# Folding the output projection ahead of the first normaliser, and holding the last band's taps until the third band

## The chip, the cores and the metric

The kernel runs on one NeuronCore of one Trainium2 chip. The metric is the device time of one execution in microseconds (us); lower is better. The engines are TensorE (PE in the profile, with its weight loads as PEld), VectorE (DVE), ScalarE (ACT), GpSimd (POOL) and SyncE (SP, which issues most DMAs).

## The reference

Eight images of 384 channels and 64 x 64 pixels, all in float32, go through two residual layers. Each layer starts with a group normalisation over 32 groups (`_gn`).

```python
# layer 0: linear attention, 6 heads of 64
q = apply_rope_2d(conv1x1(xn, Wq, bq)); k = apply_rope_2d(conv1x1(xn, Wk, bk)); v = conv1x1(xn, Wv, bv)
q = elu(to_heads(q) * scale) + 1;  k = elu(to_heads(k)) + 1
kv = einsum('bhnd,bhne->bhde', k, v);  k_sum = k.sum(axis=2)
normalizer = einsum('bhnd,bhd->bhn', q, k_sum)
out = einsum('bhnd,bhde->bhne', q, kv) / (normalizer + 1e-6)
x = x + conv1x1(out, Wfc, bfc)
# layer 1: spectral filter, depthwise convolution, gate
t = einsum('bchw,oc->bohw', _gn(x), w_in)
t = irfft2(rfft2(8x8 patches of t) * fft_filter)
t = depthwise 3x3 convolution of t with w_dw, zero-padded
x1, x2 = halves of t's channels
x = x + einsum('bchw,oc->bohw', gelu(x1) * x2, w_out)
```

## The kernel before, in words

**Tiles.** An image is held as channels on partitions: 3 tiles (CT = 3) of 128 channels. Its 4096 pixels are cut into 8 bands of 8 rows (NBAND = 8), 512 pixels each. A band of activations is a tile of 128 x 3 x 512 float32.

**Stages.** A loop runs over the images b. For each, `queries` works the second half of layer 0, band by band. Then a loop over the bands works layer 1, filled up with the keys and values of image b+1. Work is laid out with Python generators that are advanced by hand (`next`, `run`); from that the framework's scheduler makes, when the program is built, a fixed order for each engine. Engines wait for each other with semaphores.

**A band in `queries`.** These steps follow each other, and different bands are in different steps at once:
- `q_project`: TensorE makes pq (L597, 18 matmuls in two or three groups); DVE multiplies it with the tables of the rotary embedding (the "turns", L610, L625), ScalarE makes the third tile's swapped half (qs, L624), DVE adds (L626). `elu_plus_one` then is ScalarE's relu and exp (L337, L338) and a last DVE step (L339) on the tile qc.
- `q_normalise`: TensorE multiplies qc with ks_bd (pn, L635); DVE takes the reciprocal (L644) and splits it in parts for a bf16 matmul, with two casts on ScalarE (L648, L650).
- `q_spread`: TensorE spreads the parts over the channels (prb, L659), and DVE multiplies qc with them in four pieces (L668).
- `project_out`: TensorE makes pf from qc and mt (L676, in two pieces: the first 6 matmuls and the other 12), DVE adds it to x (L680).

**The fold.** The output projection needs mt, the product of the image's kv matrix (kvt) and Wfc. `kv_finish_heads` makes kvt: ScalarE copies the accumulated matrix to kx (L566), POOL puts the key sums into ks_bd with 12 small copies (L498), DVE makes kvt_bd (L571), TensorE transposes it (pt, L583), and ScalarE copies it to kvt (L584). Its last step is `fold`: TensorE makes pm (L508) and nine copies bring it to mt, five on ScalarE (L515) and four on DVE (L513). In `queries` the rest of that generator, with the fold, runs after the projection of band 2, and pn_0 is ahead of it.

**The last band of the image before.** In layer 1 a band's depthwise convolution has 3 tiles x 9 taps. The first tap is made by ScalarE (`first_taps`, L776); the other eight are DVE steps that accumulate in the tile dw (`tile_taps`, L787), 24 in a band. Then come the gate (L799 to L804) and `contraction` (pw, L820 and L831), whose result ScalarE copies to y (L845) and POOL adds into the output in DRAM with an accumulating DMA (L850). Band 7 of image b-1 is not finished in its own stage: `last_band` is a generator, handed to `queries(b)` as `late`. Each `next(late, None)` in the loop over j (from j = 2 on) is one step: the taps of tile 0, of tile 1, of tile 2 with the gate, and the contraction. The weights are in `w_dw`, in SBUF since the start, so the scheduler is free to start these DVE steps as soon as DVE has room; in the order that it made, 13 of the 24 taps of band 7 stand between 985 and 1013 us of the profile, among the steps of bands 0, 1 and 2. There are seven such boundaries, one for each image but the first.

**Buffers.** The band tiles qc, qs, kx, kvt and others come from one pool of 9 (`w_tile`); a new tile waits for the last use of the one that it replaces. The tiles dw come from a pool of two. PSUM has eight tiles (`ps_tile`).

**Loads.** x of the image after comes through SP's queue in the order in which it is written; bands 0 and 1 are loaded at j = 5 and j = 6 of `queries`.

Of the kernel before, what the change touches and what calls it, by code (L numbers as in the profile page):

```python
# [9 lines left out]
F32 = mybir.dt.float32  # L10
BF16 = mybir.dt.bfloat16
AF = mybir.ActivationFunctionType
ALU = mybir.AluOpType

P = 128
C = 384
CT = 3
H = W = 64
N = H * W
NBAND = 8  # L20
# [97 lines left out]
def conv_blocks_kernel(ctx: ExitStack, tc: tile.TileContext, a: dict, out: bass.AP, nb: int):  # L118
    nc = tc.nc
# [6 lines left out]
    small = ctx.enter_context(tc.tile_pool(name="small", bufs=2))  # L126
    psum = ctx.enter_context(tc.tile_pool(name="psum", bufs=8, space=bass.MemoryType.PSUM))

    def ps_tile(name):
        return psum.tile([P, 512], F32, tag="ps", name=name)  # L130

    def w_tile(shape, name):
        return work.tile(shape, F32, tag="w", name=name)
# [6 lines left out]
    def load_x(b, j):  # L140
        if b >= nb:
            return
        t = xp.tile([P, CT, BT], F32, tag="x", name=f"x_{b}_{j}")
        nc.sync.dma_start(t, x_in[b][:, :, j * BT : (j + 1) * BT])
        xt[b, j] = t
# [96 lines left out]
    ident = groups[:, 2 * CT * NG :]  # L242
# [4 lines left out]
    scale = HD ** -0.5  # L247
# [9 lines left out]
    ring = []  # L257
# [245 lines left out]
    def fold(b, kvt, wfc, done):  # L503

        mt = small.tile([P, CT, C], F32, tag="mt", name=f"mt_{b}", bufs=1)
        for t in range(CT):
            pm = ps_tile(f"pm_{b}_{t}")
            nc.tensor.matmul(pm[:, :C], kvt[:, t, :], wfc[:, t, :], start=True, stop=True)  # L508
            for i, (c, at, n) in enumerate(QPIECES):
                if c // P == t:  # L510
                    dst, src = mt[at % P : at % P + n, at // P, :], pm[c % P : c % P + n, :C]
                    if i % 2:
                        nc.vector.tensor_copy(dst, src)  # L513
                    else:
                        nc.scalar.copy(dst, src)  # L515
        done.append(mt)
# [113 lines left out]
    def q_normalise(b, j, q):  # L630

        pn = ps_tile(f"pn_{b}_{j}")
        for t in range(CT):
            for s in range(4):
                nc.tensor.matmul(  # L635
                    pn[32 * s : 32 * s + 32, :P],
                    ks_bd[:, t, :],
                    q[:, t, s * P : (s + 1) * P],
                    start=(t == 0),
                    stop=(t == CT - 1),  # L640
                )
        rn = small.tile([P, P], F32, tag="rn", name=f"rn_{b}_{j}")
        nc.vector.tensor_scalar_add(rn, pn[:, :P], 1e-6)
        nc.vector.reciprocal(rn, rn)  # L644

        part = small.tile([P, P], BF16, tag="part", name=f"part_{b}_{j}")
        parts = small.tile([P, P], BF16, tag="parts", name=f"parts_{b}_{j}")
        nc.scalar.copy(part, rn)  # L648
        nc.vector.scalar_tensor_tensor(rn, part, take_off[:, 0:1], rn, ALU.mult, ALU.add)
        nc.scalar.copy(part, rn)  # L650
        nc.vector.scalar_tensor_tensor(parts, part, take_off[:, 1:2], rn, ALU.mult, ALU.add)
        return parts

    def q_spread(b, j, q, rn):
        pr = [ps_tile(f"prb_{b}_{j}_{s}") for s in range(4)]
        for t in range(CT):
            for s in range(4):
                strip = slice(32 * s, 32 * s + 32)
                nc.tensor.matmul(  # L659
                    pr[s][:, t * P : (t + 1) * P],  # L660
                    expand[strip, t * P : (t + 1) * P],
                    rn[strip, :],
                    start=True,
                    stop=True,
                )
        for s in range(4):
            qq = q[:, :, s * P : (s + 1) * P]
            nc.vector.tensor_mul(qq, qq, pr[s][:, :C].rearrange("p (t n) -> p t n", t=CT))  # L668
# [80 lines left out]
    dw, dw_pe, diagonals = {}, {}, []  # L749

    def on_array(b, j):

        return b == nb - 1 and j >= NBAND - 2
# [7 lines left out]
    def array_taps(b, j, ks):  # L761

        for k in ks:
            nc.tensor.matmul(
                dw_pe[b, j].rearrange("p (r w) -> p r w", w=W),
                diagonals[0][:, k * P : (k + 1) * P],
                ring[j % 2][:, 2, k // 3 : k // 3 + 8, k % 3 : k % 3 + W],
                start=(k == 0),
                stop=(k == 8),
            )  # L770

    def first_taps(b, j):

        acc = dw[b, j] = taps_pool.tile([P, CT, 8, W], F32, tag="dw", name=f"dw_{b}_{j}")
        for m in range(CT - on_array(b, j)):
            nc.scalar.activation(acc[:, m], ring[j % 2][:, m, 0:8, 0:W], AF.Copy, scale=w_dw[:, m, 0:1])  # L776
        if on_array(b, j):
            dw_pe[b, j] = ps_tile(f"ptap_{b}_{j}")
            array_taps(b, j, range(9 if j == NBAND - 1 else 6))

    def tile_taps(b, j, m):

        t, acc = ring[j % 2], dw[b, j]
        for k in range(1, 9):
            src = t[:, m, k // 3 : k // 3 + 8, k % 3 : k % 3 + W]
            wd = w_dw[:, m, k : k + 1]
            nc.vector.scalar_tensor_tensor(acc[:, m], src, wd, acc[:, m], ALU.mult, ALU.add)  # L787

    def taps(b, j):
        if on_array(b, j) and j < NBAND - 1:  # L790
            array_taps(b, j, range(6, 9))
        for m in range(CT - on_array(b, j)):
            tile_taps(b, j, m)

    def gate_taps(b, j):
        g = gated
# [58 lines left out]
    def layer0_chain(b, prepared):  # L855

        if b >= nb:
            return
        wk = load_weight(b, "wk", k_runs) if b else first_wk
        params = []  # L860
        if b == 0:
            sum_weight(wk, "wk")
        yield from norm_chain(b, 0, params)
        scale_weight(wk, params)
        yield
        prepared += params, wk, k_bias(b, params)
# [5 lines left out]
    def run(*chains):  # L872

        chains = list(chains)
        while chains:
            chains = [c for c in chains if next(c, chains) is not chains]
# [65 lines left out]
    def queries(b, keys, before_last, late):  # L942


        wq, qbias = keys.wq, keys.qbias
        q, done, normaliser = {}, [], {}

        def normalise(j):
            normaliser[j] = q_normalise(b, j, q[j])

        run(q_project(b, 0, wq, qbias, q))
        before_last()
        run(keys.accumulate(NBAND - 1))
        finish = keys.finish(done)
        for _ in zip(q_project(b, 1, wq, qbias, q), finish):
            pass
        prepared = []
        chain = layer0_chain(b + 1, prepared)

        normalise(0)  # L960
        run(q_project(b, 2, wq, qbias, q))
        run(finish)
        mt = done[0]
        q_spread(b, 0, q[0], normaliser.pop(0))
        project = q_project(b, 3, wq, qbias, q)
        next(project)
        normalise(1)
        run(project)
        output_ = project_out(b, 0, q.pop(0), mt)
        next(output_)  # L970
        q_spread(b, 1, q[1], normaliser.pop(1))
        normalise(2)
        run(output_)
        for j in range(2, NBAND):
            if j < NBAND - 2:
                project = q_project(b, j + 2, wq, qbias, q)
                for _ in range(2):
                    next(project)
                normalise(j + 1)
                run(project)  # L980
                next(chain, None)
            q_spread(b, j, q[j], normaliser.pop(j))
            output_ = project_out(b, j - 1, q.pop(j - 1), mt)
            if j == NBAND - 2:
                next(output_)
                normalise(j + 1)
            run(output_)
            if j < NBAND - 2:
                next(chain, None)
            if j == 5:  # L990
                load_x(b + 1, 0)
            next(late, None)
            if j == 6:
                load_x(b + 1, 1)
        run(chain)
        run(project_out(b, NBAND - 1, q.pop(NBAND - 1), mt))
        return prepared
# [14 lines left out]
    for c0, at, n in QRUNS:  # L1012

        t, p0, quarter, first = at // P, at % P, c0 // QC, c0 % QC
# [13 lines left out]
    w_dw = const_tile([P, CT, 9], "w_dw", a["w_dw"], nc.sync)  # L1028
# [30 lines left out]

    def last_band(b):  # L1060

        for m in range(CT):
            tile_taps(b, NBAND - 1, m)
            if m == CT - 1:
                gate_taps(b, NBAND - 1)
            yield
        if b + 1 < nb - 1:
            contract(b, NBAND - 1)

    before_last, late = nothing, iter(())  # L1070
    for b in range(nb):
# [52 lines left out]
        def before_last(b=b):  # L1124
            contract(b, NBAND - 2)

        late = last_band(b)


    make_diagonals()  # L1130
    b = nb - 1
# [60 lines left out]
```

## Time and profile before

| | before |
|---|---|
| time, median of 3 runs | 3383.83 us (3383.71 to 3386.06) |
| the profiled execution: time, span | 3384.08 us, 3382.3 us |
| mean granted TensorE clock | 0.992 of full speed |
| PE busy | 3300.6 us |
| DVE busy | 2786.1 us |
| ACT busy | 1965.9 us |
| POOL busy | 142.6 us |
| fold's copies on DVE (L513), one | 551 ns |
| fold's copies on ACT (L515), one | 472 to 475 ns |
| a tap on DVE (L787), one | 748 ns |
| a first tap on ACT (L776), one | 756 ns |
| y's accumulating DMA, 768 KB, issue to landing | 7.8 us median, 7.6 to 9.6 |
| loading of an activation table on ACT, one | 1.28 us |

A row of a group reads: line, engine, operation, output and inputs with their shapes, count, busy time and mean duration of one, and then the idle time of the engine just before these instructions, with the instruction that ended it. A row of the list of waits reads: what waited, what it waited for, microseconds in total, how often, the longest. A row of the timeline reads: start, duration, instruction, count, and the idle time before it. Durations on one engine overlap by some 0.08 us, so that a tap of 748 ns takes 0.66 us of DVE's time in a row of taps. In rows by windows, the number behind POOL is the granted clock of TensorE.

### The profile page before, as it was taken

The numbers are of one execution on the slowest core, as the hardware profiler recorded it, in microseconds if no ns is written. First come the engines' busy times: TensorE is split into PE (matmuls) and PEld (weight loads), VectorE is DVE, ScalarE is ACT, GpSimd is POOL, SyncE is SP. The second block draws the span as 40 slices with busy tenths as digits, with TensorE's granted clock in tenths as the row PEclk, the third lists the DMA queues.
The fourth block names the chain that finished last, engine by engine and source line by source line (L and its number), as shares of the span: only waits on it lengthen the run. The fifth ranks groups of instructions, "written<-read, shape, count | busy, mean of one in ns | idle before, by whom it ended". The sixth has DMA issues, their size and how long they took to land.

```text
span 3382.3 us, 53235 instructions
## 1 busy us (share of the span) xinstructions
PE 3300.6 (98%) x21356; PEld 1850.2 (55%) x21356; DVE 2786.1 (82%) x4438; ACT 1965.9 (58%) x3849; POOL 142.6 (4%) x247
## 2 busy tenths in 40 slices
PE   8999999999999999999999999999999999999987
PEld 5544565456654566545664456644566445664454
DVE  6587889968899688996889868898788977989598
ACT  4445675556665576655675556655576555555553
POOL 0000001000010000100001000010000100000000
PEclk9999999999999999999999999999999999999999
DMA  6323244242442423424334333433233431324113
GB/s 223 112 94 108 75 101 111 100 138 56 111 115 94 135 74 87 123 101 120 85 89 122 102 115 76 111 109 116 92 96 93 120 114 54 85 70 112 57 24 53
DMA packets 149483, 336.01 MB, mean 99 GB/s; under 512 B 27140, under 2 KB 38388, under 8 KB 141044
## 3 DMA queue, kind: packets, MB, share of 16 engines
q1 hardware_dynamic: 123844, 282.85, 24.9%
q0 software_dynamic: 25200, 49.55, 10.1%
q8 instruction: 168, 2.75, 0.3%
q14 instruction: 79, 0.65, 0.1%
q10 hardware_dynamic: 192, 0.21, 0.0%
HBM read 232.70 MB, written 99.88 MB: 98 GB/s over the span
## 4 chain that ended last, share of the span: by engine, by line
PE 82%; DVE 14%; ACT 2%; issue 1%; DMA 0%; SPq 0%; DVEq 0%; ACTq 0%
PE pf L676 15%; PE pk L438 14%; PE pi L694 13%; PE pv L454 13%; PE pq L597 9%; DVE dw L787 6%; PE pw L820 4%; PE pb L729 3%; PE pd L708 2%; PE pw L831 2%; PE acc L470 2%; PE acc L483 2%; PE pn L635 1%; DVE qc L610 1%; DVE qc L339 1%
## 5 line engine op out<-in xcount | busy, mean ns | idle before, releaser
L787 DVE SCALAR_TENSOR_TENSOR dw<-ring,w_dw,dw 128x512 f32<-128x512 f32 x1520 | 1063.1, 748 | 244.2 <-ACT ring L745 205.4
L597 PE MATMUL pq<-x,wq 128*128 128x512 f32 x1152 | 529.0, 607 | 27.9 <-ACT qs L624 16.9
L438 PE MATMUL pk<-wk,x 128*128 128x384 f32 x1536 | 543.6, 495 | 0.0
L694 PE MATMUL pi<-w_in,hf 128*128 128x384 f32 x1536 | 514.4, 492 | 1.3 <-ACT hf L332 1.3
L676 PE MATMUL pf<-qc,mt 128*128 128x512 f32 x1152 | 512.8, 598 | 0.2
L454 PE MATMUL pv<-wv,x 128*128 128x384 f32 x1344 | 470.0, 488 | 0.0
L694 PEld LDWEIGHTS pi<-w_in,hf 128*128 128x128 f32 x1536 | 288.4, 191 | 196.0 <-issue 3.8
L438 PEld LDWEIGHTS pk<-wk,x 128*128 128x128 f32 x1536 | 282.9, 190 | 204.6 <-issue 31.3
L597 PEld LDWEIGHTS pq<-x,wq 128*128 128x128 f32 x1152 | 213.0, 192 | 278.9 <-issue 241.1
L461 ACT COPY v<-pv 128x384 f32<-128x384 f32 x224 | 108.7, 485 | 423.9 <-PE pv L454 416.3
L454 PEld LDWEIGHTS pv<-wv,x 128*128 128x128 f32 x1344 | 253.6, 190 | 181.4 <-issue 8.4
L676 PEld LDWEIGHTS pf<-qc,mt 128*128 128x128 f32 x1152 | 213.6, 190 | 253.7 <-issue 238.8
L680 DVE SCALAR_TENSOR_TENSOR x<-pf,bfc,x 128x512 f32<-128x512 f32 x192 | 140.8, 744 | 121.4 <-PE pf L676 121.3
L337 ACT ACTIVATE qs<-qc 128x1536 f32<-128x1536 f32 x64 | 95.0, 1485 | 169.7 <-DVE qc L626 148.6
L820 PE MATMUL pw<-gated,w_out 128*128 128x256 f32 x768 | 179.9, 384 | 0.0
L441 DVE TENSOR_TENSOR kc<-pk,kbias 128x384 f32<-128x384 f32 x256 | 141.0, 551 | 38.5 <-PE pk L438 38.2
L179 ACT ACTIVATE differences<-x,shift 128x512 f32<-128x512 f32 x168 | 119.7, 713 | 86.4 <-DVE x L680 86.4
L701 ACT COPY ht<-pi 128x384 f32<-128x384 f32 x256 | 115.0, 482 | 92.0 <-PE pi L694 88.7
L820 PEld LDWEIGHTS pw<-gated,w_out 128*128 128x128 f32 x768 | 146.9, 192 | 37.1 <-issue 6.5
L624 ACT ACTIVATE qs<-pq,qbias 64x512 f32<-64x512 f32 x128 | 87.4, 683 | 123.8 <-DVE qc L610 122.6
L850 POOL DMA_DIRECT2D out_dram<-y x63 | 80.7, 1281 | 1849.0 <-ACT y L845 847.1
L337 ACT ACTIVATE ks<-kc 128x1536 f32<-128x1536 f32 x64 | 95.0, 1485 | 98.6 <-DVE kc L445 69.5
(171 smaller groups left out, 4360.9 us busy)
## 6 DMA issues: line engine op xcount, KB each, us to landing
tq<-in_tq SPq DMA_DIRECT2D x64, 1024.0 KB, 4.8
x<-in_x SPq DMA_DIRECT2D x64, 768.0 KB, 5.9
tk<-in_tk SPq DMA_DIRECT2D x64, 768.0 KB, 4.4
out_dram<-x SPq DMA_DIRECT2D x63, 768.0 KB, 3.3
out_dram<-y POOLq DMA_DIRECT2D x63, 768.0 KB, 7.8
xs<-in_x SPq DMA_DIRECT2D x56, 768.0 KB, 5.9
wk<-in_wk SPq DMA_DIRECT2D x8, 576.0 KB, 3.8
wfc<-in_wfc SPq DMA_DIRECT2D x8, 576.0 KB, 7.9
```

The source lines that it names most:

```text
L179: nc.scalar.activation(out[:, m, :], x_[:, m, :], AF.Identity, bias=shift[:, m : m + 1], accum_out=of_m[0])
L337: nc.scalar.activation(e, x_, AF.Relu, scale=-1.0)
L438: nc.tensor.matmul(pk[:, :C], tokens(t), wks[:, t, :], start=(t == 0), stop=(t == CT - 1))
L441: nc.vector.tensor_add(kc[:, i, :], pk[:, :C], bias)
L454: nc.tensor.matmul(pv[:, :C], xt[b, j][:, t, i * P : (i + 1) * P], wvs[:, t, :], start=(t == 0), stop=(t == CT - 1),)
L597: nc.tensor.matmul(p_, wqs[:, t, m * P : (m + 1) * P], xt[b, j][:, t, :], start=(t == 0), stop=(t == CT - 1),)
L676: nc.tensor.matmul(p_, mt[:, t, m * P : (m + 1) * P], q[:, t, :], start=(t == 0), stop=(t == CT - 1))
L680: nc.vector.scalar_tensor_tensor(xm, p_, bfc[:, m : m + 1], xm, ALU.add, ALU.add)
L694: nc.tensor.matmul(p_[:, :C], h[:, t, i * P : (i + 1) * P], w_in[:, t, :], start=(t == 0), stop=(t == CT - 1),)
L701: nc.scalar.copy(ht[:, i, :], p_[:, :C])
L787: nc.vector.scalar_tensor_tensor(acc[:, m], src, wd, acc[:, m], ALU.mult, ALU.add)
L820: nc.tensor.matmul(p_[h][:, m - m0, :], w_out[:, 0, m * P : (m + 1) * P], gated[:, h * HT : (h + 1) * HT], start=(m == m0), stop=False,)
```

## The change

- The fold is run ahead of `normalise(0)`, for every image but the first; its nine copies are all made by ScalarE then.
- Four of band 7's 24 DVE taps (taps 1 and 2 of tiles 1 and 2) are made by ScalarE, each pair as a scaled copy into a tile of the `w_tile` pool, and added to dw by an accumulating DMA that POOL issues, from SBUF to SBUF, 512 KB each.
- The other taps are held: `late` has new first steps. Two of them are the added taps, and the third makes a copy of the weights by way of TensorE and DVE (`pwd`, `late_w`); the last tap of tile 0 and all that are left of tiles 1 and 2 read this copy, so that they can't be made before it, at band 3.
- `late` is advanced twice before the loop over j, and has one step more; gate and contraction come one band later (j = 5 and j = 6). Band 1 of the next image's x is loaded at j = 7 instead of j = 6.

```diff
@@ fold @@
-                    if i % 2:
+                    if i % 2 and not b:
                         nc.vector.tensor_copy(dst, src)
                     else:
                         nc.scalar.copy(dst, src)
@@ layer 1 @@
+    first_on_vector = {}
+
+    def add_tap(b, j, k, m0):
+
+        t = w_tile([P, CT, 8, W], f"tap_{b}_{j}_{k}")
+        for m in range(m0, CT):
+            nc.scalar.activation(t[:, m], ring[j % 2][:, m, 0:8, k : k + W], AF.Copy, scale=w_dw[:, m, k : k + 1])
+            first_on_vector[b, j, m] = k + 1
+        nc.gpsimd.dma_start(out=dw[b, j][:, m0:], in_=t[:, m0:], accum_op=ALU.add)
+
...
-    def tile_taps(b, j, m):
+    def tile_taps(b, j, m, weights, ks=None):
 
         t, acc = ring[j % 2], dw[b, j]
-        for k in range(1, 9):
+        for k in ks or range(first_on_vector.pop((b, j, m), 1), 9):
             src = t[:, m, k // 3 : k // 3 + 8, k % 3 : k % 3 + W]
-            wd = w_dw[:, m, k : k + 1]
+            wd = weights[:, m, k : k + 1]
             nc.vector.scalar_tensor_tensor(acc[:, m], src, wd, acc[:, m], ALU.mult, ALU.add)
...
-            tile_taps(b, j, m)
+            tile_taps(b, j, m, w_dw)
@@ queries @@
         run(keys.accumulate(NBAND - 1))
+        next(late, None)
         finish = keys.finish(done)
         for _ in zip(q_project(b, 1, wq, qbias, q), finish):
             pass
         prepared = []
         chain = layer0_chain(b + 1, prepared)
 
+        next(late, None)
+        if b:
+            run(finish)
         normalise(0)
         run(q_project(b, 2, wq, qbias, q))
         run(finish)
...
-            if j == 5:
-                load_x(b + 1, 0)
+            if j in (5, 7):
+                load_x(b + 1, j // 6)
             next(late, None)
-            if j == 6:
-                load_x(b + 1, 1)
@@ last_band @@
+        for k in (1, 2):
+            add_tap(b, NBAND - 1, k, 1)
+            yield
+
+        ps = ps_tile(f"pwd_{b}")
+        nc.tensor.matmul(
+            ps[:, : CT * 9], ident, w_dw.rearrange("p t k -> p (t k)"), start=True, stop=True
+        )
+        late_w = small.tile([P, CT, 9], F32, tag="late_w", name=f"late_w_{b}", bufs=1)
+        nc.vector.tensor_copy(late_w, ps[:, : CT * 9].rearrange("p (t k) -> p t k", t=CT))
+        yield
         for m in range(CT):
-            tile_taps(b, NBAND - 1, m)
+            if m == 0:
+                tile_taps(b, NBAND - 1, m, w_dw, range(1, 8))
+                tile_taps(b, NBAND - 1, m, late_w, range(8, 9))
+            else:
+                tile_taps(b, NBAND - 1, m, late_w)
             if m == CT - 1:
                 gate_taps(b, NBAND - 1)
             yield
```

## The prediction

> **What bounds the kernel now.** I read first the busy line and the shares of the chain that ended last, on the page; then TensorE's list of waits; then its timeline at one boundary between images (image 2, 985 to 1034 us); then the granted clock there. From the page:
>
> ```profile
> span 3382.3 us, 53235 instructions
> ...
> PE 3300.6 (98%) x21356; PEld 1850.2 (55%) x21356; DVE 2786.1 (82%) x4438; ACT 1965.9 (58%) x3849; POOL 142.6 (4%) x247
> ...
> PE 82%; DVE 14%; ACT 2%; issue 1%; DMA 0%; SPq 0%; DVEq 0%; ACTq 0%
> ...
> L787 DVE SCALAR_TENSOR_TENSOR dw<-ring,w_dw,dw 128x512 f32<-128x512 f32 x1520 | 1063.1, 748 | 244.2 <-ACT ring L745 205.4
> ...
> L850 POOL DMA_DIRECT2D out_dram<-y x63 | 80.7, 1281 | 1849.0 <-ACT y L845 847.1
> ```
>
> TensorE is busy for 98%. The change removes no matmul (it adds seven small ones), so all it can win is TensorE's idle time, 3382.3 − 3300.6 = 82 us, and time at a lowered clock. The chain's 14% on DVE says that DVE does end some waits; the list of waits says which (us in total, times, longest):
>
> ```profile
> PE pq L597 <- ACT qs L624: 16.9, 7, 2.5
> PE pb L729 <- DVE tf L716: 13.3, 7, 2.8
> PE pq L597 <- DVE qc L668: 11.0, 7, 2.0
> ...
> PE pn L635 <- DVE qc L339: 6.8, 7, 1.0
> ...
> PE pt L583 <- DVE kvt_bd L571: 3.3, 13, 0.3
> ```
>
> Four of them, 16.9 + 11.0 + 6.8 + 3.3 = 38.0 us, lie at the seven boundaries where band 7's taps of the last image are made inside `queries` of the next. The one on tf lies elsewhere and stays. One boundary on TensorE (start, duration, idle before):
>
> ```profile
> 1001.49 1.05 PE L635 MATMUL pn<-qc,ks_bd 128*32 128x128 f32 x24 [0.96 <-DVE qc L339]
> ...
> 1015.26 2.84 PE L597 MATMUL pq<-x,wq 128*128 128x512 f32 x6 [2.50 <-ACT qs L624]
> 1018.04 0.86 PE L635 MATMUL pn<-qc,ks_bd 128*32 128x128 f32 x24
> 1020.94 7.11 PE L597 MATMUL pq<-x,wq 128*128 128x512 f32 x12 [2.04 <-DVE qc L668]
> ...
> 1031.63 2.84 PE L676 MATMUL pf<-qc,mt 128*128 128x512 f32 x6
> ```
>
> The reader is to see three gaps, of 0.96, 2.50 and 2.04 us, and that the 12 pq matmuls at 1020.94 take 7.11 us, where five other boundaries show 5.42. The clock tells why (TensorE's granted clock is the column after POOL): after the same gap it fell here and did not at the next boundary.
>
> ```profile
> 1022.00:1024.00 2.00, 2.00 (x3) 0.76 (x3) 2.00 (x3) 1.11 (x3) 0.00 (x0) 0.50 0.00 0
> ...
> 1436.00:1438.00 2.00, 2.00 (x6) 0.86 (x5) 2.00 (x3) 1.11 (x3) 0.00 (x0) 1.00 0.00 0
> ```
>
> **The boundary, part by part.** My measure is from the start of pw L831 to the start of band 0's second piece of pf (988.03 to 1031.63 above). Over the seven boundaries it is 41.91, 43.60, 41.91, 43.56, 41.92, 41.90, 40.85: 295.7 us, of which about 35.9 each is work.
>
> *Taps.* Between 985 and 1013 DVE makes 13 of band 7's taps. After the change 5 are left there: 8 × 0.66 us (their step in the timeline; 748 ns each, overlapping) = 5.3 us off DVE where it is late. 13 others go to bands 3 to 6, where DVE's own work is 12.7 us of an 18.06 us band: room for about 8 a band. Free there, but for the end of this part. Four taps of the 24 leave DVE altogether.
>
> *Fold.* Four mt copies (L513, 551 ns) go to ScalarE: 2.3 us off DVE, 4 × 0.47 = 1.9 us onto ScalarE. TensorE does pm before pn_0 instead of after pq_2. With the gate and its table load gone from ScalarE here (1.28 + 0.63 us), I walk the new order with the rows' durations, on the clock of the timeline above: kvt_bd is ready at 997.6 as before (ScalarE's kx sets it); exp of band 0 ends 998.5; elu 1000.3; pm 1000.5 to 1002.6; pn_0 1002.5 without a wait; pq_2 to 1011.2. Band 1's turns end 1003.6 (before 1005.2). ScalarE then has qs_1 to 1005.0 and seven of the mt copies to 1008.4 ahead of band 1's relu and exp, so exp ends 1011.55, elu 1013.3, band 0's parts 1013.6. TensorE is out of work at 1011.2: **a new wait of 2.4 us, before prb_0, takes the place of the three old ones**. From there nothing waits: pq_3 ends 1022.75, the second piece of pf starts 1026.5. So 38.5 us against 41.91 (four boundaries), 43.6 (two, with the clock's loss) and 40.85: 4 × 3.4 + 5.1 + 5.1 + 2.35 = **26.1 us won**.
>
> *Two taps' scalings and their transfers.* Each of two ScalarE steps is two 128x512 copies at the price of the first tap (756 ns). The first pair falls into ScalarE's idle stretch of 6.04 us before 989.45, the second behind kvt, ahead of qs_1's operands: both hidden. POOL issues each transfer in 1.28 us (L850) and is 4% busy; y_6's transfer and the ks_bd copies stand behind it, and neither is needed that early (ks_bd at 1002.06, pn_0 at 1002.5: the tightest, 0.4). DVE's write of qs_1, and so ScalarE's turn of band 1, waits for the first transfer, because its buffer comes from the same pool; behind it on DVE stand all turns of band 1 and the elu for which TensorE already waits. The issue ends at about 986, the write is due at 1000.8: a margin of 14 us. No row shows a transfer from SBUF to SBUF that adds. The nearest is y's, which adds into DRAM: 768 KB landing 7.6 to 9.6 us after issue, median 7.8. For 512 KB I take 5 to 8; the lower end is the 3.3 us of x's store (768 KB), the upper one, for a path without a row, twice y's longest, 19 us. I take y's, so nothing. [...] Here y's 63 issues took 1277 to 1416 ns beside a DVE that is busy for 82%. [...]
>
> *Weights copy.* A 128x27 matmul and its DVE copy: about 0.15 us of TensorE × 7 = 1.0 us **lost**, an estimate by prb's matmuls.
>
> *Contraction moved a band later.* In before it stands between pf_4 and pf_5's scaling and covers band 7's elu:
>
> ```profile
> 1107.87 2.75 PE L820 MATMUL pw<-gated,w_out 128*128 128x256 f32 x12
> 1110.55 1.57 PE L831 MATMUL pw<-gated,w_out 64*128 64x256 f32 x12
> ...
> 1108.74 1.75 DVE L339 SCALAR_TENSOR_TENSOR qc<-qc,qs 128x1536 f32<-128x1536 f32 x1
> ...
> 1107.19 1.47 ACT L338 ACTIVATE qs<-qs 128x1536 f32<-128x1536 f32 x1
> ```
>
> The two pw rows are 4.1 us of cover. After the change TensorE runs prb_6 and the first piece of pf_5 and comes to pn_7 at 1110.95. DVE, in its new order, has prb_6's four multiplications (1.94 us) ahead of that elu, and ScalarE's exp comes behind one more table load (1.28 us): elu runs 1110.86 to 1112.6. **A new wait of 1.65 us** at six boundaries and 0.9 at the seventh: 10.8 us **lost**. The contraction itself is only moved, and its y copies have 0.35 us to spare before pf_6. The load of x for the image after next now stands behind a store on SP's queue, lands at about 1139 and is needed at 1147: nothing. One wait of the statistics (ps_r) grows by about 0.1: 0.6 us **lost**.
>
> *Clock.* In before 4 of 13 gaps of 1.9 us or more were followed by 3.4 us at half clock, which costs 1.7 us where nothing hides it. [...] The rows show otherwise, gaps of 2.04 to 2.5 us that did trip it. I take the rows: 3 of the 7 new gaps × 1.7 = 5 us **lost** ([...]if all trip, 12).
>
> **Sum.** 26.1 − 1.0 − 10.8 − 0.6 − 5 = 8.7 us won. The profiled execution took 3384.08 us, 1.8 more than its span, and is 0.25 us above the median of the runs shown (3383.83). 3384.1 − 8.7 = 3375.4; against the median, **3375 us**. 0.2%, about what a measurement of this kernel can tell from no change, is 6.8 us: the forecast is only just past it.
>
> **Rivals.**
> - *The stall only moves.* ScalarE, now with nine copies, sets a later prb_0: 1 us more at each boundary (7), or the clock falls at every gap (7 more), or pn_7 waits 2.5 instead of 1.65 (6). For it: both new waits come out of a walk of 60 us and more with margins of tenths. Then 3378 to 3385, no change. Against: DVE's 7.6 us at the boundary are gone whatever ScalarE does. 0.25.
> - *More is won.* ScalarE's exp is not behind the seven copies, or the elu of band 7 comes before the multiplications, or no gap trips the clock: 5 to 11 us more, 3363 to 3370. Against: both orders are fixed in each engine's program. 0.15.
> - *Slower: the first added transfer lands late.* Place: DVE's first turn of band 1, due 14 us after the issue. Each us beyond is 1 us of all that follows, seven times. Break-even is 14 + 8.7/7 = 15.2 us after issue, slower by 0.2% from 16.2 us, and at 18 us it is 7 × 4 − 8.7 = 19 us lost: 3403 us. For it: no row of such a transfer[...]. Against: y's longest, 9.6 us for half as many bytes again. 0.15.
> - *The edit does not do what it says:* the held taps are pushed into bands where DVE is late. Against: no wait of TensorE falls in bands 3 to 6 in before, and DVE has 5 us of slack a band there. Within the first rival.
>
> **How the numbers follow.** The main case, 0.45, has 3369 to 3381 as its own range; about four fifths of it lie under 3377. Faster: 0.35 of it + 0.15 = 0.50. The rest of it (0.10) and most of the first rival (0.16) are no change: 0.26. The slow rival and the tail of the first one (waits and clock together, 0.09): 0.24. The range, 3363 to 3394, takes in the gain of the second rival and landings of up to about 16.7 us, and leaves out the worse ones.
>
> **What would show it.** Right: the waits on qs L624 and qc L668 before pq gone; a wait before prb of about 2.4 us, seven times, ended by DVE's parts; pn_7 waiting on DVE's qc L339 about 10 us in all; TensorE's idle 60 to 70 us; the stretch from pw to pf 38.5 us. Wrong: DVE or ScalarE waiting at qs_1 for the added transfer; TensorE waiting in bands 3 to 6 for qc or x; the stretch still at 41; no wait of pn_7.

## The result

| | before | after |
|---|---|---|
| time, median of 13 runs each | 3384.05 us (3382.58 to 3388.23) | 3376.68 us (3375.61 to 3379.08) |
| span of the profiled execution | 3382.3 us | 3374.4 us |

The ratio is 0.9977, with a 95% interval of 0.9968 to 0.9985: 7.4 us faster by the medians, 0.22%, and 7.8 us by the ratio. The forecast was 3375 us, 8.7 to 8.8 us faster.

The first lines of the page of the changed kernel, with its longest group of taps and the row of the added transfers among the DMA issues (the last number of that row is the median of us from issue to landing):

```profile
span 3374.4 us, 53258 instructions
...
PE 3299.9 (98%) x21370; PEld 1851.2 (55%) x21370; DVE 2754.2 (82%) x4389; ACT 2006.7 (59%) x3911; POOL 143.1 (4%) x261
...
PE 81%; DVE 12%; ACT 4%; issue 1%; DMA 1%; SPq 0%; DVEq 0%; ACTq 0%
...
L797 DVE SCALAR_TENSOR_TENSOR dw<-ring,w_dw,dw 128x512 f32<-128x512 f32 x1401 | 978.8, 749 | 244.0 <-ACT ring L745 205.4
...
dw<-tap POOLq DMA_DIRECT2D x14, 512.0 KB, 4.8
```

DVE lost 32 us of work and ScalarE took on 41, and TensorE, the bound, is as busy as before. What moved the time is in TensorE's list of waits (total, times, longest):

```profile
PE prb L659 <- DVE parts L651: 17.0, 7, 2.4
PE pb L729 <- DVE tf L716: 14.2, 6, 3.6
PE pn L635 <- DVE qc L339: 10.5, 7, 1.6
```

The waits of pq for qs L624 and qc L668 are gone, and so is that of pn_0: the row of pn is now that of band 7. Two others stand in their place, each once per boundary. The boundary of image 2 on TensorE's timeline, and the place of band 7's normaliser 96 us later:

```profile
1003.16 7.99 PE L597 MATMUL pq<-x,wq 128*128 128x512 f32 x18
1013.58 0.35 PE L659 MATMUL prb<-parts,expand 32*128 32x128 bf16 x12 [2.43 <-DVE parts L651]
1013.86 4.54 PE L597 MATMUL pq<-x,wq 128*128 128x512 f32 x6
...
1028.11 5.42 PE L676 MATMUL pf<-qc,mt 128*128 128x512 f32 x12
...
1109.45 0.86 PE L635 MATMUL pn<-qc,ks_bd 128*32 128x128 f32 x24 [1.57 <-DVE qc L339]
```

One gap of 2.43 us has taken the place of three, and the six pq matmuls behind it take 4.54 us where they took 2.84: the clock fell. By windows, after this gap and after the same gap of image 4 (the granted clock is the number behind POOL):

```profile
1014.00:1016.00 2.00, 2.00 (x3) 0.78 (x4) 2.00 (x5) 1.05 (x2) 0.00 (x0) 0.61 0.46 86
1016.00:1018.00 2.00, 2.00 (x4) 0.67 (x2) 1.89 (x4) 0.32 (x1) 0.00 (x0) 0.54 0.96 385
...
1838.00:1840.00 2.00, 1.84 (x16) 1.02 (x17) 2.00 (x5) 0.48 (x1) 0.00 (x0) 1.00 0.18 37
```

The first two rows follow the gap of image 2, where the clock fell; the last follows that of image 4, where it did not. It fell at four of the seven boundaries.

### The profile page after: what moved, and what is told of

Same layout as the page of the kernel before. It is cut to its first block, busy times and chain, and to the rows that moved or that the text cites. A ratio compares the mean times of both kernels' runs of the same rounds, so it can differ in the third digit from the quotient of the medians.

```text
span 3374.4 us, 53258 instructions
## 1 busy us (share of the span) xinstructions
PE 3299.9 (98%) x21370; PEld 1851.2 (55%) x21370; DVE 2754.2 (82%) x4389; ACT 2006.7 (59%) x3911; POOL 143.1 (4%) x261
## 4 chain that ended last, share of the span: by engine, by line
PE 81%; DVE 12%; ACT 4%; issue 1%; DMA 1%; SPq 0%; DVEq 0%; ACTq 0%
PE pi L694 14%; PE pk L438 13%; PE pf L676 13%; PE pv L454 13%; PE pq L597 10%; DVE dw L797 4%; PE pw L830 4%; PE pb L729 3%; PE pd L708 2%; PE pw L841 2%; PE acc L470 2%; PE acc L483 2%; PE pn L635 1%; DVE qc L610 1%; DVE qc L339 1%
## 5 line engine op out<-in xcount | busy, mean ns | idle before, releaser
L797 DVE SCALAR_TENSOR_TENSOR dw<-ring,w_dw,dw 128x512 f32<-128x512 f32 x1401 | 978.8, 749 | 244.0 <-ACT ring L745 205.4
L624 ACT ACTIVATE qs<-pq,qbias 64x512 f32<-64x512 f32 x128 | 87.3, 682 | 109.4 <-DVE qc L610 108.4
```

## The experiments

Ten kernels were timed, each beside the kernel before. The numbers of waits are TensorE's, from each run's profile. "Against before" is 3384 x (ratio - 1), so that all rows can be set side by side. The last column says at how many of the seven boundaries the granted clock fell in the profiled execution; in the kernel before it fell at four. All of these kernels but act_copies_only keep the changed place of the load of x.

| run | hold | fold | transfers | ratio (95% interval) | against before | clock fell at |
|---|---|---|---|---|---|---|
| fold_only | no | ahead, ScalarE | no | 1.0011 (1.0002 to 1.0019) | +3.7 us | 7 |
| transfers_only | no | old | yes | 1.0000 (0.9992 to 1.0008) | 0.0 | 5 |
| the changed kernel | yes | ahead, ScalarE | yes | 0.9977 (0.9968 to 0.9985) | -7.8 | 4 |
| old_fold | yes | old | yes | 0.9977 (0.9970 to 0.9985) | -7.8 | 4 |
| act_copies_only | no | old place, ScalarE | no | 0.9959 (0.9946 to 0.9971) | -13.9 | 2 |
| cover | yes, contraction a band earlier | ahead, ScalarE | yes | 0.9957 (0.9944 to 0.9969) | -14.6 | 2 |
| late_hold | yes, from a band later | ahead, ScalarE | yes | 0.9950 (0.9936 to 0.9964) | -16.9 | 3 |
| hold_only | yes | old | no | 0.9946 (0.9933 to 0.9958) | -18.3 | 2 |
| no_transfers | yes | ahead, ScalarE | no | 0.9943 (0.9931 to 0.9956) | -19.3 | 4 |
| nt_early_norm | yes | ahead, ScalarE; normaliser earlier | no | 0.9913 (0.9900 to 0.9927) | -29.4 | 0 |
| nt_late_act_fold | yes | old place, ScalarE | no | 0.9898 (0.9884 to 0.9911) | -34.5 | 0 |

### Undoing one part: cover, old_fold, no_transfers, and one part alone: fold_only

**cover.** The copy of the weights and the taps of tile 0 become one step, so that the gate comes a band earlier and the contraction of the last band goes back between pf_4 and pf_5:

```diff
         nc.vector.tensor_copy(late_w, ps[:, : CT * 9].rearrange("p (t k) -> p t k", t=CT))
-        yield
         for m in range(CT):
```

> The changed kernel, with the step of late that copies the weights joined to the taps of tile 0 (the yield between them is taken out), so that gate and contraction of the last band come one band earlier, where they stood in the kernel before. Theory (the lost cover): the contraction stands again between pf_4 and pf_5 and hides band 7's elu, so pn_7's wait for qc L339 (10.5 us in all in the changed kernel) falls under 1 us, and the time falls by 8 to 11 us against the changed kernel, to 3366 to 3369. Rival (bands too full): 13 held taps and the gate in one band less make DVE late in bands 3 to 5, TensorE waits there instead, and the time stays within 4 us of the changed kernel, 3373 to 3380.

Measured: 3370.84 us (3368.83 to 3373.41), about 7 us better than the changed kernel by the ratios. Of pn_7's seven waits one is left, of 1.1 us, but at the other six TensorE then waits for DVE's multiplications, which have slid behind the late elu:

```profile
PE pf L676 <- DVE qc L668: 6.4, 6, 1.1
```

So the uncovered elu was the cause of pn_7's wait, but the cover wins back only some 3 us of the 10.5, because elu is still late. The rest of the 7 us came with the clock: TensorE is busy for 3295.3 us instead of 3299.9, as the clock fell at two boundaries instead of four. Neither theory gave the number: bands 3 to 5 are not too full.

**old_fold.** The fold behind band 2's projection, with its copies split as before; hold and transfers stay:

```diff
         next(late, None)
-        if b:
-            run(finish)
         normalise(0)
...
-                    if i % 2 and not b:
+                    if i % 2:
                         nc.vector.tensor_copy(dst, src)
```

> The changed kernel, with the fold back in its old place (after the projection of band 2) and its copies split over ScalarE and DVE as before; taps held and two of them transferred as in the changed kernel. Theory (the fold's copies hold up ScalarE): without seven mt copies ahead of band 1's relu and exp, and with band 0's parts early on DVE, TensorE finds prb_0 ready behind pm. The wait of 2.43 us before prb is gone at seven boundaries and with it the four clock drops of 1.65 us: 17 + 6.6 = about 23 us less than the changed kernel, 3350 to 3358. Rival (the fold is what wins): DVE's four copies come back at the boundary, pn_0 or pq_3 wait as in the kernel before, 3377 to 3384.

Measured: 3377.39 us (3375.14 to 3380.47), the time of the changed kernel. prb_0 is ready behind pm, as the theory had it, but the lateness comes out one band on:

```profile
1009.89 0.34 PE L659 MATMUL prb<-parts,expand 32*128 32x128 bf16 x12
...
1024.32 0.35 PE L659 MATMUL prb<-parts,expand 32*128 32x128 bf16 x12 [1.88 <-DVE parts L651]
```

DVE had its four mt copies back, 2.2 us, and band 1's parts were late by 1.88 us. The theory's step that failed: it took the copies' place on ScalarE as the only cause and left DVE's load out. The rival's number was right and its place (pn_0 or pq_3) was not.

**fold_only.** The changed fold in a kernel whose taps are as before:

```diff
-        for k in (1, 2):
-            add_tap(b, NBAND - 1, k, 1)
+        for _ in range(2):
             yield
 
-        ps = ps_tile(f"pwd_{b}")
...
-        yield
         for m in range(CT):
-            if m == 0:
...
-                tile_taps(b, NBAND - 1, m, late_w)
+            tile_taps(b, NBAND - 1, m, w_dw)
```

> The kernel before with the fold alone: ahead of the first normaliser, its copies all on ScalarE; no tap is held or transferred, gate and contraction stand where they stood before. Theory (the held taps are what wins): 13 taps are still among DVE's steps, elu of band 1 ends about 1015.8 on the clock of the timeline shown, prb_0 waits about 4.9 us in one piece, as long as the three waits that it replaces, and trips the clock at all seven boundaries; 3380 to 3388, no gain. Rival (the fold wins by itself): the waits before pq and pn shrink to under 3 us a boundary, 3366 to 3376.

Measured: 3389.26 us (3387.23 to 3390.09), slower than before by 0.02 to 0.19%. As the theory had it, three waits became one of 4.7 us:

```profile
PE prb L659 <- DVE parts L651: 32.1, 7, 4.7
```

That is no more idle time than the 34.7 us (16.9 + 11.0 + 6.8) of before, but it is in one piece, and the clock fell behind it at all seven boundaries (TensorE busy for 3304.2 us, before 3300.6).

**no_transfers.** The changed kernel without `add_tap`; all 24 taps on DVE:

```diff
-        for k in (1, 2):
-            add_tap(b, NBAND - 1, k, 1)
+        for _ in range(2):
             yield
```

> The changed kernel without the two taps made by ScalarE and added by transfers: all 24 taps are on DVE, held as in the changed kernel. Theory: DVE's order at the boundary stays as it is (five taps there, by the built program), and bands 3 to 6 have room for the four, so the time is that of the changed kernel within 3 us, 3374 to 3380, with the same waits before prb and pn. Rival (the transfers relieve a full DVE): TensorE waits for DVE in bands 3 to 6 or longer at pn_7, 4 taps x 0.66 us x 7 = up to 18 us slower, 3385 to 3395.

Measured: 3366.75 us (3362.98 to 3367.61), 10 to 12 us **better** than the changed kernel, which neither theory had. DVE has 28 taps more, and TensorE is idle for 65.6 us instead of 74.5. The wait of 2.43 us before prb is still there, but pn_7 waits no more:

```profile
PE prb L659 <- DVE parts L651: 18.4, 8, 2.4
```

The reason is on ScalarE. Its timeline around band 7's exp (L338), the changed kernel first:

```profile
1096.08 1.28 ACT L813 ACT_TABLE_LOAD   x1
...
1104.81 1.28 ACT L338 ACT_TABLE_LOAD   x1
1106.10 1.48 ACT L338 ACTIVATE qs<-qs 128x1536 f32<-128x1536 f32 x1
```

and without transfers:

```profile
1100.72 1.47 ACT L338 ACTIVATE qs<-qs 128x1536 f32<-128x1536 f32 x1
...
1105.46 1.28 ACT L813 ACT_TABLE_LOAD   x1
```

With four taps fewer on DVE the gate's input is ready earlier, its gelu comes ahead of band 7's exp, and both have to load their table; in DVE's order the four multiplications of band 6 (L668) come ahead of elu (L339). With 24 taps the gelu comes behind the exp and elu ahead of the multiplications. DVE, the changed kernel first, then without transfers:

```profile
1105.78 1.94 DVE L668 TENSOR_TENSOR qc<-qc,prb 128x384 f32<-128x384 f32 x4
1107.64 1.76 DVE L339 SCALAR_TENSOR_TENSOR qc<-qc,qs 128x1536 f32<-128x1536 f32 x1
...
1102.27 1.75 DVE L339 SCALAR_TENSOR_TENSOR qc<-qc,qs 128x1536 f32<-128x1536 f32 x1
...
1104.60 0.55 DVE L668 TENSOR_TENSOR qc<-qc,prb 128x384 f32<-128x384 f32 x1
```

The whole kernel has 159 table loads with the transfers and 152 without. The seven are all ahead of an exp, one for each boundary (the changed kernel first):

```profile
L338 ACT ACT_TABLE_LOAD x78 | 100.1, 1283 | 1.4
...
L338 ACT ACT_TABLE_LOAD x71 | 91.1, 1283 | 1.3
```

### Is it the transfer or the gate's time? late_hold

The changed kernel with transfers and fold, but the weights' copy comes a band later, in one step with the taps of tile 0. The steps of the gate and the contraction keep their places; the held taps that lead to the gate start later:

```diff
             add_tap(b, NBAND - 1, k, 1)
             yield
 
+        yield
         ps = ps_tile(f"pwd_{b}")
...
         nc.vector.tensor_copy(late_w, ps[:, : CT * 9].rearrange("p (t k) -> p t k", t=CT))
-        yield
         for m in range(CT):
```

> The changed kernel, transfers and early fold included, with the copy of the weights made one band later and tile 0's taps joined to it; taps of tiles 1 and 2, gate and contraction stay in their steps. The held taps start a band later, so the gate and its table load come behind band 7's exp. Theory (the transfers do not cost by themselves; with four taps fewer the gate is ready too early and puts its table load and DVE's multiplications ahead of band 7's exp and elu): pn_7's wait (10.5 us in the changed kernel) falls under 1 us, the loads of tables from 159 to about 152, the time to 3364 to 3370. Rival (the transfers cost by themselves): the time stays at 3374 to 3380 whatever the gate's place.

Measured: 3366.88 us (3365.36 to 3369.48); pn_7's wait is gone from the list, and there are 146 table loads. The list begins:

```profile
PE prb L659 <- DVE parts L651: 19.4, 8, 2.4
PE pb L729 <- DVE tf L716: 13.3, 7, 2.7
```

That is the time of no_transfers (3366.75), with waits like its own: the transfers cost nothing by themselves that shows here; what cost was where they let the gate go. The same later hold without transfers was not run.

### Each of the other parts alone: hold_only, transfers_only, act_copies_only

**hold_only** is old_fold without `add_tap`; against old_fold:

```diff
-        for k in (1, 2):
-            add_tap(b, NBAND - 1, k, 1)
+        for _ in range(2):
             yield
```

> The kernel before with the hold alone: fold in its old place with its copies split over both engines, no transfers; taps held by the copied weights, contraction one band later. Theory (the hold is the whole gain; the fold moves DVE's lateness from prb_0 to prb_1, and the transfers bring pn_7's wait): the wait of 1.9 us before prb_1 stays at seven boundaries as in the run with the old fold, pn_7's wait is under 1 us, 3364 to 3370. Rival (the fold's move adds to it): 3374 or more, near the changed kernel or above.

Measured: 3365.42 us (3363.91 to 3369.72). TensorE's longest waits are these; no wait of pn_7 is in the list:

```profile
PE prb L659 <- DVE parts L651: 15.0, 8, 1.9
PE pb L729 <- DVE tf L716: 13.3, 7, 2.7
PE px L400 <- DMA x<-in_x: 6.5, 2, 6.1
```

In the list of old_fold pn_7's wait has 10.5 us, and by the ratios 10.5 us is what the transfers cost between these two kernels.

With the hold, the fold's place and the split of its copies, changed together, make no difference that can be measured (hold_only and no_transfers, 0.9946 and 0.9943). Changed one at a time they do, as nt_late_act_fold shows below.

**transfers_only** is the kernel before with the two steps of `add_tap` and no copied weights; against old_fold:

```diff
-        ps = ps_tile(f"pwd_{b}")
...
-        yield
         for m in range(CT):
-            if m == 0:
...
-                tile_taps(b, NBAND - 1, m, late_w)
+            tile_taps(b, NBAND - 1, m, w_dw)
```

> The kernel before with the four transferred taps alone: fold as before, nothing held by copied weights, contraction in its old place. By the built program 8 of band 7's taps remain among the steps of bands 0 to 2 (13 before). Theory (only DVE steps at the boundary count): 5 x 0.66 us less there, but two taps stand ahead of band 1's elu, TensorE waits about 3 us before prb_1 and the clock falls at most boundaries: 3376 to 3383. Rival (the transfers alone lose, by their own cost or their wait at the qs buffer): 3386 or more.

Measured: 3385.34 us (3381.70 to 3386.73), no change; between theory and rival. The wait before prb_1 was 1.9 us and not 3, but two waits came that the theory did not have:

```profile
PE pq L597 <- ACT mt L515: 10.0, 7, 1.4
PE pf L676 <- ACT y L855: 8.9, 6, 1.5
```

In ScalarE's timeline a table load of 1.28 us still stands ahead of band 1's exp (at 1010.69 us), as in the kernel before, and the mt copies come behind that exp; this is the first wait. The second is for ScalarE's y copies behind the contraction. It was not followed further.

**act_copies_only** is the kernel before with one edit:

```diff
-                    if i % 2:
+                    if i % 2 and not b:
                         nc.vector.tensor_copy(dst, src)
```

> The kernel before with a single edit: the fold's nine copies all on ScalarE, in their old place; taps as before. Theory (of the change's parts only DVE's load at the boundary counts, 2.2 us of copies as much as 2.2 us of taps): the wait of 2.04 us for qc L668 goes, the one for ScalarE's qs stays, 11 to 16 us less, 3368 to 3374. Rival (ScalarE then is late with mt or with band 2's exp): the wait is replaced, 3380 to 3386.

Measured: 3371.58 us (3369.18 to 3372.27). The wait for qc L668 is gone, the other two of the boundary are as before, and the clock fell at two boundaries instead of four:

```profile
PE pq L597 <- ACT qs L624: 16.7, 7, 2.5
...
PE pn L635 <- DVE qc L339: 6.7, 7, 1.0
```

### The order at the boundary: nt_early_norm, nt_late_act_fold

**nt_early_norm** is no_transfers with the fold and band 0's normaliser ahead of band 1's turns:

```diff
-        for _ in zip(q_project(b, 1, wq, qbias, q), finish):
-            pass
+        project = q_project(b, 1, wq, qbias, q)
+        for _ in range(CT):
+            next(project)
+            next(finish)
+        if b:
+            run(finish)
+            normalise(0)
+        run(project)
...
-        if b:
-            run(finish)
-        normalise(0)
+        if not b:
+            normalise(0)
```

> The hold, no transfers, the fold ahead as in the changed kernel, but band 0's normaliser is issued ahead of band 1's turns, so that DVE makes the reciprocal and the parts of band 0 in the 1.4 us in which it waits for ScalarE's qs_1. Theory (the 2.43 us before prb_0 are the place of the parts in DVE's order, behind band 1's elu, not the taps): prb_0 waits under 0.5 us, the rest of the stretch holds by some tenths, 3345 to 3354. Rival (DVE's work of the stretch is too much in any order): the wait turns up at pn_1 or prb_1 with over 1.5 us, 3360 to 3368.

Measured: 3355.11 us (3354.29 to 3356.52). prb_0 follows pq_2 without a wait, and 1.6 us turn up at pn_1, the rival's place, but the whole is 10 to 12 us better than no_transfers, just above the theory's range. The new wait is shorter than 1.8 us, and the clock fell at no boundary any more.

```profile
1008.98 0.34 PE L659 MATMUL prb<-parts,expand 32*128 32x128 bf16 x12
1009.25 2.84 PE L597 MATMUL pq<-x,wq 128*128 128x512 f32 x6
1013.73 0.86 PE L635 MATMUL pn<-qc,ks_bd 128*32 128x128 f32 x24 [1.63 <-DVE qc L339]
```

**nt_late_act_fold** is hold_only with the copies of act_copies_only: hold, fold in its old place, nine copies on ScalarE. Against no_transfers:

```diff
-        if b:
-            run(finish)
         normalise(0)
```

> The hold, no transfers, the fold in its old place behind band 2's projection, but all nine copies on ScalarE. Theory (DVE's steps and their order at the boundary set the wait, and ScalarE has room behind band 1's exp, not ahead of its relu): band 0's parts come early, DVE has no mt copy, so neither prb_0 nor prb_1 waits over 0.7 us, and the clock stays up at the boundaries: 14 + 7 = some 20 us less than the changed kernel without transfers, 3343 to 3352. Rival (the copies are then late for pq_3 or pf_0): waits of 1.5 to 2.5 us there, 3360 to 3370.

Measured: **3349.78 us** (3349.42 to 3351.25), 1.0% faster than before and 27 us better than the changed kernel. At the boundary only tenths are left, and the clock fell at none. The gains of the hold (18.3 us) and of the copies (13.9) add up: their sum is 32.2 us, and 34.5 were measured, each known to some 4 us. Against no_transfers, which differs only in the fold's place, it is 15 us better; against hold_only, which differs only in the split of the copies, 16.

```profile
1006.64 0.35 PE L659 MATMUL prb<-parts,expand 32*128 32x128 bf16 x12
1007.14 2.84 PE L597 MATMUL pq<-x,wq 128*128 128x512 f32 x6 [0.15 <-ACT mt L515]
...
1019.09 0.35 PE L659 MATMUL prb<-parts,expand 32*128 32x128 bf16 x12 [0.39 <-DVE parts L651]
```

## Why the prediction was right, and by what

- **The boundary's stretch.** From pw to the second piece of pf it is now 39.99, 40.04, 39.98, 38.34, 40.04, 38.35 and 37.62 us, 274.4 in all against 295.7: 21.3 us won. The walk's 38.5 is met where the clock held (38.34, 38.35). Its 26.1 less the clock's 5 make 21.1. Two misses cancel in this: without the clock's loss the walk would have won 27.9 us and not 26.1 (the seventh boundary came to 37.62), and the clock took 6.6 and not 5. That part of the agreement is luck.
- **The new wait before prb_0.** Forecast 2.4 us, measured 2.43, seven times. fold_only shows what it consists of: 4.7 us without the hold.
- **The clock.** Taken from the rows of before as 3 of 7 gaps at 1.7 us, measured 4 of 7 at 1.65 (40.0 against 38.35), 6.6 us instead of 5. The boundaries of before hold 12 gaps of 1.9 us or more, not 13, and nothing in the prediction said behind which gaps the clock falls: other kernels of the same change had it fall at none and at all seven.
- **pn_7 without its cover.** Forecast 10.8 us, measured 10.5. cover and no_transfers showed the mechanism as stated, the table load and the multiplications ahead of elu. The prediction put it down to the contraction's move alone, though; it was as much a consequence of where the transfers let the gate go (no_transfers, late_hold).
- **The weights' copy.** Forecast 1.0 us; the profile shows two matmuls each time and 0.25 us, 1.75 us in all. This term was a little over half of what it had to be.
- **The transfers.** Taken as free, with 5 to 8 us to landing. They landed after 4.8 us (4.5 to 5.8), and an issue took 0.90 us of POOL, beside a DVE that is busy for 82%. No wait of TensorE is put down to them, and the rival that needed 15 us or more is excluded.
- **The rest.** 21.3 − 10.5 − 1.75 = 9.05; the span fell by 7.9. The remaining 1.1 us (0.6 was forecast, for ps_r, whose waits grew by 0.2) is spread over waits of tenths (pb for tf, 13.3 to 14.2, is the largest of them) and was not taken apart.
- **A sign that failed.** TensorE's idle time was to be 60 to 70 us; it is 3374.4 − 3299.9 = 74.5. The range did not follow from the prediction's own terms: 81.7 less the three waits that go (34.7) and plus the new ones (16.8, 10.8 and 0.6) is 75.2.

The sum was right, but the change was judged as a package. Its parts alone are +4 us (fold with its copies), 0 (transfers) and −18 (hold), the first and the last together −19, and all three −8: they don't add, because each changes what the others wait for.

The fold is itself two edits that cancel. With the hold, nine copies on ScalarE take the time from −18 to −34.5 (hold_only, nt_late_act_fold), and the fold's move ahead of the normaliser brings it back to −19 (no_transfers). Without the hold the same steps give −14 (act_copies_only) and then +4 (fold_only). So the move, by which the change is named, cost 15 to 18 us both times. The prediction did not weigh it apart from the copies.

What of the hold's gain comes from the eight taps that leave the boundary, and what from the gate with its table load, which leaves with them, no run separates: transfers_only took five taps away there, left the gate, met two new waits, and gained nothing.

## What to carry to other kernels

Where an engine is late for the one that bounds the kernel, count all of its steps up to the point of waiting, and then their order: taking steps away moved the gap, and only fewer steps together with a better order (parts before elu, copies behind exp) closed it. Work taken off an engine also makes what follows it ready earlier, and an operation that needs another activation table can then slip ahead of one that is urgent; the transfers lost 10 us that way with less work on DVE. When several edits come together, run each alone: here the hold and the copies on ScalarE held a gain of 34 us, and the fold's move and the transfers took more than three quarters of it back.

## What was not expected of the hardware

The clock did not fall behind every gap of one length. In the changed kernel the gap before prb is 2.42 to 2.44 us at all seven boundaries. The granted clock was 0.50 behind four of these gaps, for 3.41 us each time (from 601.42, 1014.43, 1427.44 and 2250.05 us), and 1.00 behind the other three (from 1838.16, 2661.09 and 3070.98 us). In the kernel before it was 0.50 for 3.41 us as well, at four boundaries (from 1021.18, 1847.21, 2256.81 and 3079.42 us).

The runs in order of their longest gap at a boundary, each from its profiled execution (for cover, where the clock fell at two, no row above shows the gap):

| run | longest gap at a boundary | clock fell at |
|---|---|---|
| nt_late_act_fold | tenths | 0 |
| nt_early_norm | 1.6 us | 0 |
| old_fold | 1.9 us | 4 |
| hold_only | 1.9 us | 2 |
| transfers_only | 1.9 us | 5 |
| the changed kernel | 2.4 us | 4 |
| late_hold | 2.4 us | 3 |
| no_transfers | 2.4 us | 4 |
| before | 2.5 us, with a second of 2.0 us at five | 4 |
| act_copies_only | 2.5 us | 2 |
| fold_only | 4.7 us | 7 |

Over all twelve profiled executions, 19 of the 47 gaps of 2 to 2.5 us at the boundaries were followed by half clock, at up to another 1.65 us each. One profile of each kernel is read here, and the lengths rest on matmul ends, which are modelled in the profile. What decides between gaps of one length was not tested.
